# An attention kernel's norm sums, small columns and last-tile order are rearranged

## The chip, the core and the metric

The kernel runs on one core of a Trainium2 chip. The core has five engines that run side by side, each through its own list of instructions in order: TensorE (PE in the profile) multiplies matrices, VectorE (DVE) and ScalarE (ACT) work on elements, GpSimd (POOL) as well, and SyncE (SP) issues the transfers. The metric is the device time of one execution in microseconds.

## The reference

Text rows x (4 x 2048 x 512) attend to a short context (4 x 77 x 384). Cut to what matters:

```
text_p  = x @ W_text + b_text
audio_p = ctx @ W_audio + b_audio
Q = layer_norm(text_p, g1, beta1);  K = layer_norm(audio_p, g2, beta2);  V = audio_p
alpha = softmax(Q K^T / sqrt(512))
h = alpha V W_out + b_out
out = layer_norm(h + x, g_out, beta_out)
```

All is float32.

## The kernel before

Text rows are handled in 64 tiles of 128. Instead of projecting x and then multiplying with the keys, the kernel prepares one matrix for each batch entry, `mu`, which holds W_text (with its mean removed) times the scaled keys, and beside them the Gram matrix of W_text in a form that gives the square |t|^2 of the projected, centred row as a product with x itself. A tile's projection `y` (PE, L428) therefore holds the raw scores and, in further columns, the vector whose product with x is |t|^2. The Gram part of the last chunk of columns goes into a small bank of its own, `yl` (L436). The values are folded with W_out into `vw`, so that the tile's output is one product `h` (L515) of the turned weights `et` and `vw`.

The steps of a tile are named by a letter in the order lists:

- `x` turns a tile of x on DVE (L379), from a buffer `xq` that SP loads in a spread form (L178; two such buffers, each for four tiles, loaded when the tile with t == 2 begins its projection). The plain rows of x for the residual are loaded by SP too (L166, when t == 0).
- `p` and `P` are the two halves of the projection on PE. `p` does chunks 3 and 2, with `yl` after the first; `P` does 1 and 0. There are two `y` banks and two `yl` banks.
- `s` (score, DVE): adds `uws` to the scores (L463) and sums the first three chunks of |t|^2 (L452). `t` (score_rest) adds the last chunk's share from `yl` (L452), from which the final `ss` comes.
- `r` is the inverse root of |t|^2 (POOL: a maximum, L478, and a power, L209), `c` scales the scores and takes their maximum (DVE, L485 and L488), `e` the exponential (ACT, L495), `w` and `W` the transposes of the weights (PE, L507), into whichever `yl` bank the next projection will use, and their copy by ACT (L508).
- `a` is the product h (PE), `i` the reciprocal of the sum (DVE), `z` the residual sum with its row sum (DVE, L528), `q` the sum of squares (ACT, L536), `d` the inverse deviation `ro` (the scaled negative mean `nm` on ACT, L544; a multiply and add on POOL, L545; a power on POOL, L209).
- The final norm is done in one of two ways. On DVE, `v`, two operations (L559 writes an intermediate into a used `y` bank, L560 applies scale and offset and the row is stored). Or by `o` (shift `no` = nm * ro, DVE, L567), `y` (ACT, L572) and `m` (two operations of POOL, L576 and L577), after which the row is stored.

Steps r, c, e, w, i, d and o are done for a batch of tiles at once: four in most of the run, then seven batches of two and two of one. Thirteen buffers hold `z`; one comes free when its row is stored.

A front stage loads the weights, forms the keys and values in three blocks of rows (77, 128 and 103), centres W_text (`centre(k)`, k = 0 and 2 on DVE, 1 and 3 on ACT), turns it and makes the Gram matrix. `keep_warm` issues transposes of an identity matrix that have no other use. Then 40 tiles run in a regular loop, in which later steps of earlier tiles are mixed into each tile's projection (slot), and the last 24 in an order written out by hand. Every engine runs its instructions in the order in which the program emits them, SP's loads and stores included:

```
in_program_order(tc)
```

## Time and profile before

| what | value |
|---|---|
| time, median of 3 runs | 300.28 us (299.94 to 300.8) |
| the profiled execution | 301.12 us |
| its span, from first to last instruction | 299.4 us |
| mean granted TensorE clock | 0.989 |
| busy share PE / DVE / ACT / POOL | 95% / 78% / 47% / 54% |
| bytes moved | 55.58 MB, mean 186 GB/s |

The profile is of one execution. Its own time exceeds its span, as something is done around the first and last instruction. A busy share is a mean over the whole span, so stages are read by stretches. A row of the timeline has the start, the length, the engine and line, what is written and read, the shape, and in brackets how long the engine was idle before and what released it. The lines "L428" and so on are those of the kernel above; the changed kernel's lines are a few higher.

### The profile page before, as it was taken

To read this page: it belongs to the slowest core of one execution; us is meant where nothing else is said; L and a number is where in the kernel's file an instruction comes from. 1 tells how busy PE (TensorE), PEld (TensorE's weight loads), DVE (VectorE), ACT (ScalarE), POOL (GpSimd) and SP (SyncE) were. 2 spreads that over 40 slices of the span, in tenths; PEclk is the share of its full clock that TensorE was granted. 3 is DMA by queue.
4 is the path that set the end of the run, shared out by engine and by line. 5 is a ranking of instruction groups with operands and counts; after the bars stand their busy time and mean duration, and the time that the engine had idled before them with its cause. 6 is when DMAs were issued, how large, how long until landed. Compare 5 with 4: busy or idle time off the path is not lost.

```text
span 299.4 us, 3953 instructions
## 1 busy us (share of the span) xinstructions
PE 284.5 (95%) x1016; PEld 167.4 (56%) x1016; DVE 234.1 (78%) x733; ACT 139.5 (47%) x409; POOL 161.4 (54%) x188
## 2 busy tenths in 40 slices
PE   8899999999999999999999999999999999999950
PEld 6385755555555655555555555565645555556520
DVE  0593243567869798989898989889899998999985
ACT  2466210032345464636373736463656556527471
POOL 0011000010117667767585868599887887876774
PEclk9999999999999999999999999999999999999995
DMA  5999805359391878788879695969895969210315
GB/s 180 264 278 349 249 8 98 58 169 166 138 252 43 172 248 162 260 162 264 171 250 186 237 194 227 208 240 219 278 227 210 246 238 209 106 71 36 112 51 191
DMA packets 54282, 55.58 MB, mean 186 GB/s; under 512 B 2585, under 2 KB 35673, under 8 KB 54259
## 3 DMA queue, kind: packets, MB, share of 16 engines
q1 hardware_dynamic: 54259, 55.33, 68.5%
q8 instruction: 8, 0.13, 0.2%
q14 instruction: 15, 0.12, 0.1%
HBM read 38.23 MB, written 16.78 MB: 184 GB/s over the span
## 4 chain that ended last, share of the span: by engine, by line
PE 81%; DMA 6%; DVE 6%; SPq 2%; issue 1%; ACT 1%; POOL 0%; ACTq 0%; DVEq 0%
PE y L428 45%; PE h L515 17%; PE yl L436 4%; PE vw_ps L358 3%; PE m_ps L315 3%; PE et_ps L507 2%; DMA ca<-in_ctx_dram 2%; PE w_ps_yl L608 2%; DMA xq<-in_x_dram 2%; DMA out_dram<-z 2%; PE va_ps L253 2%; SPq L178 2%; DVE y L452 1%; PE w_ps_y L608 1%; DVE y L559 1%
## 5 line engine op out<-in xcount | busy, mean ns | idle before, releaser
L428 PE MATMUL y<-mu,xt 128*128 128x464 f32 (+2 forms) x512 | 178.8, 473 | 0.0
L428 PEld LDWEIGHTS y<-mu,xt 128*128 128x128 f32 x512 | 89.9, 190 | 50.0 <-issue 34.4
L515 PE MATMUL h<-vw,et 77*128 77x512 f32 x128 | 63.9, 596 | 1.3 <-ACT et L508 1.2
L536 ACT ACTIVATE sqj<-z,sz 128x512 f32<-128x512 f32 x64 | 46.1, 720 | 36.6 <-DVE z L528 33.1
L576 POOL TENSOR_TENSOR z<-z,go 128x512 f32<-128x512 f32 x44 | 55.7, 1267 | 13.8 <-ACT z L572 13.7
L577 POOL TENSOR_TENSOR z<-z,beo 128x512 f32<-128x512 f32 x44 | 55.8, 1268 | 3.4
L528 DVE SCALAR_TENSOR_TENSOR z<-h,inv,x 128x512 f32<-128x512 f32 x64 | 46.6, 733 | 2.8 <-PE h L515 1.9
L379 DVE STREAM_TRANSPOSE xt<-xq 128x512 f32<-128x512 f32 x64 | 44.6, 702 | 0.1
L452 DVE CUSTOM_DVE_ANT_1 y<-y,x,e 128x384 f32<-128x384 f32 x64 | 40.1, 626 | 2.3
L478 POOL TENSOR_SCALAR rs<-ss 128x4 f32<-128x4 f32 (+2 forms) x21 | 4.7, 223 | 68.4 <-DVE ss L452 51.3
L572 ACT ACTIVATE z<-z,no,ro 128x512 f32<-128x512 f32 x44 | 35.0, 806 | 10.4 <-DVE no L567 10.3
L436 PEld LDWEIGHTS yl<-ub,xt 128*128 128x128 f32 x128 | 23.6, 188 | 26.2 <-issue 12.6
L508 ACT COPY et<-et_ps 77x256 f32<-77x256 f32 (+1 forms) x33 | 11.9, 362 | 51.3 <-PE et_ps L507 51.3
L463 DVE TENSOR_TENSOR e<-y,uws 128x80 f32<-128x80 f32 x64 | 15.1, 235 | 18.4 <-PE y L428 18.2
L515 PEld LDWEIGHTS h<-vw,et 77*128 77x128 f32 x128 | 23.2, 190 | 10.6 <-issue 4.9
L495 ACT ACTIVATE e<-e,mx 128x77 f32<-128x77 f32 x64 | 22.2, 350 | 13.7 <-DVE mx L488 13.6
L452 DVE CUSTOM_DVE_ANT_1 yl<-yl,x,sa 128x128 f32<-128x128 f32 x64 | 22.7, 354 | 3.5
L436 PE MATMUL yl<-ub,xt 128*128 128x128 f32 x128 | 24.5, 273 | 0.0
L209 POOL TENSOR_TENSOR rs<-rs,mhalf 128x4 f32<-128x4 f32 (+2 forms) x21 | 18.6, 886 | 1.8
L209 POOL TENSOR_TENSOR ro<-ro,mhalf 128x4 f32<-128x4 f32 (+2 forms) x21 | 18.2, 867 | 1.8
L507 PEld LDWEIGHTS et_ps<-ident,e 128*77 128x77 f32 x64 | 9.1, 147 | 15.0 <-issue 9.3
L560 DVE SCALAR_TENSOR_TENSOR z<-y,ro,beo 128x512 f32<-128x512 f32 x20 | 15.0, 751 | 0.9
(102 smaller groups left out, 241.5 us busy)
## 6 DMA issues: line engine op xcount, KB each, us to landing
xq<-in_x_dram SPq DMA_DIRECT2D x64, 256.0 KB, 5.4
x<-in_x_dram SPq DMA_DIRECT2D x16, 1024.0 KB, 7.7
out_dram<-z SPq DMA_DIRECT2D x64, 256.0 KB, 2.4
wc<-in_L_xattn_W_text_dram SPq DMA_DIRECT2D x2, 512.0 KB, 8.7
wo<-in_L_xattn_W_out_dram SPq DMA_DIRECT2D x1, 1024.0 KB
wa<-in_L_xattn_W_audio_dram SPq DMA_DIRECT2D x3, 256.0 KB, 2.6
ba<-in_L_xattn_b_audio_dram SPq DMA_DIRECT2D x1, 256.0 KB, 6.7
bo<-in_L_xattn_b_out_dram SPq DMA_DIRECT2D x1, 256.0 KB
```

The costliest lines, as they stand in the source:

```text
L209: nc.gpsimd.tensor_tensor(dst, v, mhalf[: v.shape[0], : v.shape[1]], ALU.pow)
L379: nc.vector.transpose(xt.rearrange("p k (a j) -> p a k j", j=R), xq[i][:, t].rearrange("p a (k i) -> p a k i", i=R),)
L428: nc.tensor.matmul(parts(y[:, : Q * AQ])[:, :, cols], lhsT=xt[:, k, :], rhs=mub[:, k, :, cols], start=(k == LAST_K), stop=(k == 0),)
L436: nc.tensor.matmul(b, lhsT=xt[:, k, :], rhs=ub.rearrange("p q i -> p (q i)"), start=True, stop=True)
L452: nc.vector.tensor_tensor_reduce(out=y, in0=y, in1=x, scale=1.0, scalar=first, op0=ALU.mult, op1=ALU.add, accum_out=to)
L495: nc.scalar.activation(e, e, AF.Exp, bias=s.mx[:, c], accum_out=s.inv[:, c])
L515: nc.tensor.matmul(s.h[n], lhsT=s.et[:, n - s.tiles[0], :], rhs=s.vw, start=True, stop=True)
L528: nc.vector.scalar_tensor_tensor(z, s.h.pop(n), s.inv[:, c], xs[i][:, t, :], ALU.mult, ALU.add, accum_out=s.sz[:, c])
L536: nc.scalar.activation(junk, s.z[n], AF.Square, bias=s.sz[:, c], scale=-float(H), accum_out=s.sq[:, c])
L572: nc.scalar.activation(z, z, AF.Identity, bias=s.no[:, c], scale=s.ro[:, c])
L576: nc.gpsimd.tensor_tensor(z, z, go, ALU.mult)
L577: nc.gpsimd.tensor_tensor(z, z, beo, ALU.add)
```

## The change

- The first chunk of W_audio is loaded from ACT's queue. The bias `ba` is loaded after the first half of W_text, where it stood before the third key block.
- A tile of zeros, set by DVE, feeds two first matmuls; of 16 warming transposes 9 remain. The three value products, the turning of the third key block and `centre(0)` and `centre(1)` are put in another order.
- `t` becomes `score_last`: it runs during the tile's own projection, and starts its sum from `bc2` (to which H * EPS is added once), writing it into the column of `uws` that `s` then adds to the scores. `s` makes the final sum `ss`; the column `sa` goes.
- `nm` is a step `n` of its own. The multiply and add of `d` moves from POOL to ACT; the shift `no` moves from DVE to ACT, one instruction for a column.
- The norm on DVE becomes two steps, `v` and `V`, which may stand apart. If the `y` bank scored last is still in use by such a pair, the one before is used.
- The order of the last 24 tiles is rewritten. The same numbers of tiles are normed in each way (13 by DVE, 23 by ACT and POOL in that list), but partly other tiles; the loads and stores follow their steps.

```diff
@@ -129,20 +129,20 @@
     wad = w_audio.rearrange("(k p) h -> p k h", p=P)
 
     def load_audio(k):
-        nc.sync.dma_start(out=wa[:, k], in_=wad[:, k])
+        (nc.sync if k else nc.scalar).dma_start(out=wa[:, k], in_=wad[:, k])
 
     load_keys(0)
     load_audio(0)
     load_keys(1)
     for k in range(1, NA):
         load_audio(k)
-    ba = load("ba", [P, H], b_audio.partition_broadcast(P))
     for i in range(2, len(key_blocks)):
         load_keys(i)
 
     wc = xqs.tile([P, ND, T, P], F32, tag="xq", name="wc").rearrange("p k t c -> p k (t c)")
     wcd = w_text.rearrange("(k p) h -> p k h", p=P)
     nc.sync.dma_start(out=wc[:, :2], in_=wcd[:, :2])
+    ba = load("ba", [P, H], b_audio.partition_broadcast(P))
     nc.sync.dma_start(out=wc[:, 2:], in_=wcd[:, 2:])
 
     vec_rows = const.tile([3 * NH, P], F32, name="vec_rows")
@@ -190,10 +190,14 @@
     beo = load("beo", [P, H], beta_out.partition_broadcast(P))
     spread_x(1)
 
+    zeros = const.tile([P, P], F32, name="zeros")
+    nc.vector.memset(zeros, 0.0)
     ident = const.tile([P, P], F32, name="ident")
     make_identity(nc, ident)
     mhalf = const.tile([P, T], F32, name="mhalf")
     nc.gpsimd.memset(mhalf, -0.5)
+    eps = const.tile([P, 1], F32, name="eps")
+    nc.gpsimd.memset(eps, EPS)
     warm = const.tile([P, T], F32, name="warm")
     nc.scalar.activation(warm, mhalf, AF.Exp)
 
@@ -340,8 +344,7 @@
                     pu[v * HP : (v + 1) * HP].rearrange("p (b s) -> p b s", s=S),
                 )
         nc.vector.memset(uws[:, :, 0, S:], 0.0)
-        for b in range(B):
-            nc.vector.tensor_scalar_add(uws[:, b, 0, S : S + 1], bc2, H * EPS)
+        nc.vector.tensor_scalar_add(bc2, bc2, H * EPS)
 
     vw = [
         batch.tile([P if b < 2 else S, H], F32, name=f"vw_{b}") for b in range(B)
@@ -390,7 +393,7 @@
         start += size
     batch_of = {n: tiles for tiles in batches for n in tiles}
 
-    ys, state, kept, scored_y = {}, {}, [], []
+    ys, state, kept, scored_y, in_bank = {}, {}, [], [], {}
     begun = [-1]
 
     class Batch:
@@ -405,7 +408,7 @@
             def columns(name):
                 return small.tile([P, T], F32, name=f"{name}_{f}", tag=name)
 
-            self.sa, self.ss, self.rs = map(columns, ("sa", "ss", "rs"))
+            self.ss, self.rs = map(columns, ("ss", "rs"))
             self.mx, self.inv = map(columns, ("mx", "inv"))
             self.sz, self.sq, self.ro, self.nm = map(columns, ("sz", "sq", "ro", "nm"))
             self.z = {}
@@ -453,23 +456,27 @@
             out=y, in0=y, in1=x, scale=1.0, scalar=first, op0=ALU.mult, op1=ALU.add, accum_out=to
         )
 
+    def score_last(n):
+
+
+        i, t = divmod(n, T)
+        s, c = of(n)
+        yl = parts(ys[n][1])
+        sum_of_products(
+            yl, parts(xs[i][:, t, :])[:, :, LAST_K * R :], bc2, s.uw[:, 0, S : S + 1]
+        )
+
     def score(n):
 
         i, t = divmod(n, T)
-        scored_y[:] = ys[n][:1]
-        y = parts(ys[n][0][:, : Q * AQ])
+        y = ys.pop(n)[0]
+        scored_y.append(y)
+        y = parts(y[:, : Q * AQ])
         s, c = of(n)
         e = s.e[:, n - s.tiles[0], :]
         nc.vector.tensor_tensor(parts(e), y[:, :, :SQ], parts(s.uw[:, 0, :]), ALU.add)
         xp = parts(xs[i][:, t, :])[:, :, : LAST_K * R]
-        sum_of_products(y[:, :, SQ:], xp, e[:, S : S + 1], s.sa[:, c])
-
-    def score_rest(n):
-
-        i, t = divmod(n, T)
-        s, c = of(n)
-        yl = parts(ys.pop(n)[1])
-        sum_of_products(yl, parts(xs[i][:, t, :])[:, :, LAST_K * R :], s.sa[:, c], s.ss[:, c])
+        sum_of_products(y[:, :, SQ:], xp, e[:, S : S + 1], s.ss[:, c])
 
     def row_scale(f):
 
@@ -537,13 +544,16 @@
             junk, s.z[n], AF.Square, bias=s.sz[:, c], scale=-float(H), accum_out=s.sq[:, c]
         )
 
+    def minus_mean(f):
+        s = state[f]
+        nc.scalar.mul(s.nm[:, : s.m], s.sz[:, : s.m], -1.0 / H)
+
     def deviations(f):
 
         s = state[f]
         m = s.m
-        nc.scalar.mul(s.nm[:, :m], s.sz[:, :m], -1.0 / H)
-        nc.gpsimd.tensor_scalar(
-            s.ro[:, :m], s.sq[:, :m], float(H) ** -3, EPS, ALU.mult, ALU.add
+        nc.scalar.activation(
+            s.ro[:, :m], s.sq[:, :m], AF.Identity, bias=eps, scale=float(H) ** -3
         )
         rsqrt(s.ro[:, :m], s.ro[:, :m])
 
@@ -551,20 +561,26 @@
         rows = out.rearrange("b l d -> (b l) d")
         nc.sync.dma_start(out=rows[n * P : (n + 1) * P, :], in_=of(n)[0].z[n])
 
-    def norm_on_vector(n):
+    def norm_on_vector(n, step):
+
+
         s, c = of(n)
         z = s.z[n]
-
-        zc = scored_y[0]
-        nc.vector.scalar_tensor_tensor(zc, z, s.nm[:, c], kept[1] if kept else go, ALU.add, ALU.mult)
-        nc.vector.scalar_tensor_tensor(z, zc, s.ro[:, c], beo, ALU.mult, ALU.add)
-        store(n)
+        if step == 0:
+            y = scored_y[-2 if any(b is scored_y[-1] for b in in_bank.values()) else -1]
+            in_bank[n] = y
+            nc.vector.scalar_tensor_tensor(y, z, s.nm[:, c], kept[1] if kept else go, ALU.add, ALU.mult)
+        else:
+            nc.vector.scalar_tensor_tensor(z, in_bank.pop(n), s.ro[:, c], beo, ALU.mult, ALU.add)
+            store(n)
 
     def norm_shift(f):
 
         s = state[f]
         s.no = small.tile([P, T], F32, name=f"no_{f}", tag="no")
-        nc.vector.tensor_tensor(s.no[:, : s.m], s.nm[:, : s.m], s.ro[:, : s.m], ALU.mult)
+        for q in range(s.m):
+            c = slice(q, q + 1)
+            nc.scalar.mul(s.no[:, c], s.nm[:, c], s.ro[:, c])
 
     def norm_on_scalar(n):
         s, c = of(n)
@@ -622,20 +638,23 @@
         nc.vector.tensor_copy(ub if k == LAST_K else u[:, :, k * R :], p[:, :, k * R :])
         nc.gpsimd.tensor_copy(mu[1][:, k, :, SQ : SQ + m], u)
 
-    keep_warm(8)
+    for i in range(2):
+        nc.tensor.matmul(four[3][:, :P], lhsT=zeros, rhs=zeros, start=True, stop=True)
+    keep_warm(6)
     context_turned(0)
-    keep_warm(8)
+    keep_warm(3)
     pv = {0: value_product(0, [0])}
     context_turned(1)
     value_product(0, range(1, NA), pv[0])
-    context_turned(2)
+    centre(0)
+    centre(1)
     for i in range(1, NB):
-        if i > 1:
-            centre(1)
-        pv[i] = value_product(i)
+        pv[i] = value_product(i, range(2))
+        if i + 1 < NB:
+            context_turned(i + 1)
+        value_product(i, range(2, NA), pv[i])
         value(i - 1, pv[i - 1])
         if i == 1:
-            centre(0)
             statistics(0)
     centre(2)
     centre(3)
@@ -722,7 +741,7 @@
         p=begin_project,
         P=end_project,
         s=score,
-        t=score_rest,
+        t=score_last,
         r=row_scale,
         c=scale_scores,
         e=exponential,
@@ -732,11 +751,13 @@
         a=apply,
         z=residual,
         q=squares,
+        n=minus_mean,
         d=deviations,
         o=norm_shift,
         y=norm_on_scalar,
         m=norm_on_gpsimd,
-        v=norm_on_vector,
+        v=lambda n: norm_on_vector(n, 0),
+        V=lambda n: norm_on_vector(n, 1),
     )
 
     def run(steps, n):
@@ -750,13 +771,13 @@
 
     for n in range(40):
         t = n % T
-        run([("p", 0), ("s", 1), ("t", 1), ("P", 0)], n)
+        run([("p", 0), ("s", 1), ("t", 0), ("P", 0)], n)
         on_vector = t == T - 1
         if not on_vector:
             run([("o", 12)] * (t == 0) + [("y", 12)], n)
         if t == 0:
             run([("r", 4)], n)
-        run([("v" if on_vector else "m", 12)], n)
+        run([("v", 12), ("V", 12)] if on_vector else [("m", 12)], n)
         if n == KEPT:
             keep()
         else:
@@ -768,36 +789,39 @@
         run([("a", 6)], n)
         run({1: [("w", 5)], 2: [("W", 6)]}.get(t, []), n)
         run([("q", 7)], n)
-        run({0: [("e", 4)], 2: [("d", 10)]}.get(t, []), n)
+        run({0: [("e", 4)], 2: [("n", 10), ("d", 10)]}.get(t, []), n)
 
 
     for step in """
-        o28
-        p40 s39 z33 y28 y29 a34 t39 a35 r36 z34 P40 c36
-        p41 m29 s40 y31 x42 t40 P41 m31
-        p42 z35 y30 P42 q33 q34 s41 q35 e36 t41 d32 w36 m28 x43
-        p43 s42 P43 o32 t42 a36 y35 i36 v33 x44 y32 a37 s43
-        p44 x46 m30 t43 W36 P44 r40 z36 z37 a39 m32 a38 x45 c40 s44 y34 z39
-        p45 P45 t44 q37 z38 e40 x47
-        p46 q36 s45 x48 q39 P46 m35 t45 q38 s46 w40 d36 i40 o36 m34 y38
-        p47 P47 t46 W40 v36 a40 y37 s47 z40 a42 t47 a43 z42 x50 x49 a41 z41 z43 q42 q40 m38 y39
-        p48 q41 r44 P48 c44 q43 m37 s48
-        p49 d40 t48 e44 x51 w44 v43 P49 W44 a45 m39 a47 o40 s49
-        p50 y41 i44 x52 t49 m41 z45 P50 z47 a46 q45 v42 z46 a44 y40 s50 q47 z44 x53 t50 r48 q46 m40
-        p51 P51 c48 s51
-        p52 t51 q44 d44 e48 o44 y45 x54 r50 i48 m45 P52 w48
-        p53 P53 s52 a48 y46 c50 t52 e50 a49 x55 v47 m46 s53 y44 i50 z48 t53 w50
-        p54 P54 x56 q48 z49 s54 a51 a50 z51 r52
-        p55 z50 q49 m44 t54 c52 q51 x57 P55 q50 d48 d50 o48 s55 e52 i52 o50
-        p56 t55 v50 y48 w52 P56 s56 a52 m48 r54 a53 y49
-        p57 z52 m49 t56 y51 z53 c54 q52 P57 x58 q53 e54 w54
-        p58 x59 a55 d52 s57 t57 o52 P58 v52 r56 i54 c56 y53 x60
-        p59 s58 z55 t58 P59 e56 a54 w56 s59 i56 z54
-        p60 t59 m53 P60 x61 m51 a57 r58 a56 q54 q55 x62 c58 s60 d54 o54 z57 e58 y54
-        p61 z56 m54 t60 v55 q57 w58 P61 i58 q56 a59 d56 a58 s61 x63
-        p62 t61 o56 y57 P62 z58 z59 r60 m57
-        p63 q59 c60 s62 P63 e60 v56 q58 t62 s63 i60 d58 o58 w60 t63 a60 r62 c62 z60 a61 r63 y59 e62 w62 i62
-        c63 e63 a62 q60 z61 i63 w63 z62 v58 a63 q61 q62 m59 z63 d60 o60 d62 v60 v62 q63 y61 d63 m61 v63
+        s39 z33
+        p40 r36 o28 P40 x42 t40 y30 a35 z35 s40 a34 c36 y31 z34 x43
+        p41 y28 P41 m30 t41 n32 s41
+        p42 m31 P42 t42 m28 x44 q34 s42 e36 w36
+        p43 q33 x45 q35 P43 t43 a37 d32 s43
+        p44 v35 o32 r40 i36 y33 W36 V35 z37 a36 y34 y29 c40 q37 m33 P44 z36 m29 y32 a38 t44 z38 q36 x46 e40
+        p45 s44 m34 q38 a39 P45
+        p46 P46 z39 t45 n36 q39 s45 t46 d36 x47 x48 w40 i40 s46
+        p47 a41 o36 y38 v37 t47 x49 W40 z41 a40 y36 y39 V37 z40 P47 s47 a42 a43
+        p48 m32 m38 P48 q41 z42 q40
+        p49 q42 r44 x50 z43 q43 t48 n40 c44 m36 d40 s48 v41 e44 w44 P49 a45 t49 o40 x51 V41 m39 y43 a44 W44 i44
+        s49 z44 r48 z45
+        p50 t50 y42 q44 a47 x52 c48 q45 z47 P50 e48 a46 q47 m43 s50 z46 v40 m42 q46
+        p51 w48 n44 P51 t51 d44 V40
+        p52 i48 s51 v47 a49 o44 a48 x54 x53 r50 y46 P52 y45 m46 y44 V47 c50 t52 z48
+        p53 e50 z49 q48 w50 q49 P53 s52 m44 a51 t53 n48 d48 a50 s53 i50
+        p54 o48 y48 r52 x55 P54 z50 z51 m45 t54
+        p55 c52 P55 s54 n50 q51 q50 d50 m48 x57 e52 x56 w52 o50
+        p56 t55 x58 s55 P56 y51 v49 r54 i52 t56 V49 a53 x59 c54 a52
+        p57 y50 e54 z52 z53 m51 w54 P57 i54 s56 a54 a55 m50 t57
+        p58 q53 x60 s57 q52 n52 z55 d52 r56 z54 P58
+        p59 o52 t58 y52 c56 q55 s58 v53 e56 i56 q54 w56 P59 n54 a57 m52 d54 t59 o54 V53 y54 y55 s59 a56 z57 r58
+        z56 q56 q57 m54
+        p60 c58 x61 t60 P60 x62 n56 d56 e58
+        p61 s60 w58 v56 i58 t61 V56 P61 o56 a59 s61 y57 a58
+        p62 x63 P62 m55 r60 m57 z59 z58 t62 q59
+        p63 n58 c60 q58 d58 s62 v58 t63 e60 r62 w60 i60 V58 c62 o58 P63 s63 a60 e62 w62 r63 z60 i62 y59 a61 q60
+        z61 a62 n60 c63 q61 z62 e63 d60 w63 n62 a63 v60 i63 v61 V60 z63 q62 m59 V61 d62 v62 n63 v63 q63 V62 d63
+        V63
     """.split():
         do[step[0]](int(step[1:]))
 
```

## The prediction

> **What bounds the kernel now.** I read the busy shares first, then the busy time by stretch, then what PE waited for, then the chain of waits and the timeline at both ends. The page:
>
> ```profile
> PE 284.5 (95%) x1016; PEld 167.4 (56%) x1016; DVE 234.1 (78%) x733; ACT 139.5 (47%) x409; POOL 161.4 (54%) x188
> PE 81%; DMA 6%; DVE 6%; SPq 2%; issue 1%; ACT 1%; POOL 0%; ACTq 0%; DVEq 0%
> ```
>
> PE's share is an average, so the stretches decide (start:end, length, then PE, PEld, DVE, ACT, POOL busy):
>
> ```profile
> 0.00:10.00 10.00, 7.65 (x28) 4.87 (x28) 0.21 (x1) 2.32 (x4) 0.74 (x7) 1.00 0.66 225
> 150.00:180.00 30.00, 30.00 (x108) 17.82 (x107) 26.78 (x84) 15.66 (x45) 21.16 (x22) 1.00 0.82 219
> 270.00:280.00 10.00, 10.00 (x35) 5.64 (x34) 9.49 (x32) 6.02 (x18) 6.76 (x11) 1.00 0.22 82
> 290.00:299.40 9.40, 0.00 (x0) 0.00 (x0) 5.77 (x10) 2.13 (x8) 4.51 (x7) 0.66 0.45 167
> ```
>
> From about 24 us to 283 us PE has no room. Time can be won in four places only: before 24 us, in the few gaps of PE, in the last dependent steps, and behind PE's last matmul (9.4 us without PE). PE's gaps for a weight transpose are these two, at 67 and 255 us, and in front of the second stands one DVE instruction:
>
> ```profile
> 67.18 0.41 PE L507 MATMUL et_ps<-ident,e 128*77 128x128 f32 x2 [0.46 <-DVE ss L452]
> 255.81 0.41 PE L507 MATMUL et_ps<-ident,e 128*77 128x128 f32 x2 [0.72 <-DVE ss L452]
> 254.24 1.09 DVE L567 TENSOR_TENSOR no<-nm,ro 128x2 f32<-128x2 f32 x1
> 255.25 0.35 DVE L452 CUSTOM_DVE_ANT_1 yl<-yl,x,sa 128x128 f32<-128x128 f32 x1
> ```
>
> The transposes write a yl bank, which comes free only when the |t|^2 rest of the tile before has been summed; that sum stood behind a 2-column `no` of 1.09 us. The end of the chain of waits, in order of time:
>
> ```profile
> 284.79 1.99 PE h L515 x4
> 288.67 0.54 ACT sqj L536
> 290.52 0.75 DVE z L528 x2
> 292.90 0.77 DVE y L559
> 293.76 0.76 DVE z L560
> 294.62 0.77 DVE y L559
> 295.48 0.75 DVE z L560
> ```
>
> These are DVE steps of 0.75 us every 0.86 us. The last ends at 296.23, and the span 3.17 us later (store and closing).
>
> **What PE must do.** A projected tile takes 0.78 + 0.22 + 1.70 = 2.70 us (chain: "y x2", "yl x2", "y x6"), an h product 0.86, a pair of transposes 0.22. At 195.85 there are left 1.70 + 23 x 2.70 + 28 x 0.86 + 14 x 0.22 = 90.96 us, so 286.81 without a gap. Before, 4 h and 2 pairs (3.88) come after tile 63's projection, whose gapless end is 282.93; the timeline has it at 281.70 + 1.86 = 283.56. Hence 0.63 us of gaps from 195 us on. PE work is unchanged, except for five warming matmuls fewer at the start.
>
> **The change part by part.**
>
> Front. ba goes behind the third key block and wc's first half; wa's first chunk goes to ACT's queue. SP's issues ahead of those two loads fall by two and by one of 0.43 us, and ba's 256 KB no longer stand ahead of wc. At the 370 GB/s that the stretch 8 to 10 us shows, that is 0.7 us: wc's first half, first used at 11.48 now, lands about 10.8. [...] Against it: DVE's centre(0) now precedes value(0), which used to fill DVE's idle time at 9.79. From 11.48 to 22.5 DVE works almost without a break, and the key transposes of PE (22.53) wait for its last `kn`. So 0.7 us are gained and value(0)'s 0.69 are put into the row: 0. PE does two chunks of the second value product while the third key block is on its way (it idled 1.00 us at 10.33), but ACT turns that block only after centre(1) (1.75 us: 10.8 to 12.5, copied by 12.95). Its six matmuls of 0.43 end at 15.5, where PE now turns wc at 15.4 to 15.8. Front: 0, bounds -0.5 and +0.8 (wc no earlier). Fewer warming transposes: they run every 0.22 us at the start and every 0.11 at 6.56, so PE is slow until about 6 us. Were it slow until 8, six matmuls would cost 0.43 more each, in time in which PE waits for loads anyway.
>
> |t|^2 of the last chunk, summed during a tile's own projection (t beside s). Same two DVE sums per tile. The waits: t stands behind yl of its own tile, 1.2 us into the slot, while s is done after 0.9, so DVE idles up to 0.3 us, with x, z and c behind it. Per four tiles DVE's work is x 4 x 0.65, s 4 x 0.82, t 4 x 0.31, z 4 x 0.67, c 1.35, v and V 1.5: 12.7 of PE's 14.68 us, so the idle time fits. At 67 us the exponential no longer has t (0.36) in front of its norm: 0.36 of the 0.46 us gap goes. At 255 the bank is free a slot earlier and `no` is not on DVE: 0.72 shown, all within the 0.63 of gaps.
>
> Small columns by ACT. `no` leaves DVE: 19 instructions, median 159 ns, but 249 and 283 in the means (3.0 + 2.0 us) and twice 0.75 and 1.09. ACT gets 60 columns and 21 `ro`, at 0.19 alone and 0.09 in a row (two `nm`: 0.28): 8 to 15 us on 139.5 (47 to about 52%). POOL loses 21 x 0.19 = 4.0. [...] By the row of `nm` (192 ns) ACT is no dearer here than DVE's mean, and ACT is not the bound. [...] I take the row: 0 beyond the `no` counted above.
>
> Norm in two steps. Between v and V the y bank is held, so two tiles later p waits for V. Tightest: tile 40 (V40 after t51, p52 behind P51): t51 and V40 take 1.1 us from yl51, P51 leaves 1.9. Tile 47: s51, v, two x and V need 3.9 us, PE has 4.4. No stall, with 0.5 us to spare. The gain: v and V of different tiles alternate. Dependent ones stand 0.86 us apart now (292.90, 293.76, 294.62), two independent residuals 0.67 (278.25, 278.92); I take 0.70. [...]
>
> Reordered loads and stores. SP's order is that of the stores, which wait for POOL or V (13 stores waited 37.9 us for POOL's z). x47 is now turned late in slot 46, and SP, which stands at p46 with the next spread load, waits for it. Its four issues (3.4 us) and the landing (5.4 us) make 8.8 us; the first use, x52 in slot 50, is over three slots (some 12 us) later. That fits with about 3 us to spare; a store that holds SP longer than that would cost PE the excess, and is left to the range. z buffers (13) return at least five slots ahead, but for z45, which needs m32's store from slot 48.
>
> The last tiles, from the end E of tile 63's projection (its gapless end is 286.81 - 3.66 = 283.15, as transposes 60 and 61 now come before). DVE up to E has t63 done and c62 nearly (ends E + 0.25); s63 to 1.07, z60 1.74, i62 1.82, z61 2.65 (h61 at 1.95), c63 3.17, z62 3.84, v60 4.53. ACT: e62 to 0.75, its copy 1.4, y59 2.2, q60 3.0, n60 3.2, q61 4.0, and only then e63 to 4.45; so transpose 4.75, copy 5.1, h63 6.1. DVE: i63 4.65, v61 5.34, V60 6.2 (POOL's power ends 5.45), z63 6.9, V61 7.6, v62 8.3, v63 9.0, V62 9.7, V63 10.5. POOL's m59 (2.54, from 5.45 to 8.0) and both powers after it (to 9.2) precede V62 and V63. Store and closing 3.17: span = E + 13.7. Before it is 283.56 + 15.84. So the tail is 2.15 us shorter: t63, i60 and two `no` leave DVE's row (0.75), the rest is pitch and waits.
>
> Sum: E = 283.15 - 0.36 (67 us) + 0 (front) + 0.3 (gaps that I allow) = 283.1. Span 296.8 against 299.4: -2.6. The profiled execution took 301.12 (1.72 around its span), the median of three is 300.28; -2.6 on that gives 297.7.
>
> **The rivals.** First: the order of the last 24 tiles stalls PE. In slots 57 to 61 DVE has 17.1 us of work in 17.6 of PE. By my walk m52, the power for 54, r58, c58 and e58 follow each other, e58 ending at 274.25 where PE wants transpose 58 at 274.6: 0.4 us to spare. POOL's m steps are 2.54 us each; if one such step comes before the r of a batch in more places than I walked, each of nine batches can lose that. This decides from 3.5 us of added gaps (2.6 + 0.9); at 4 us the time is 301.7. For it: DVE at 9.49 of 10 and in-order queues. Against it: the old order, as tightly loaded, shows 0.63. [...] Third: everything fits, no gaps, the front gains 0.5: 296.9; or 296.3, if e63 is not held up by q61.
>
> **How the numbers follow.** About 0.3% (0.9 us) is what a measurement tells from no change: 299.4 to 301.2. The forecast with its small misses, 296.9 to 299.3: 0.62; third rival 0.12; second 0.12 (of which 0.08 lies within 0.3%, 0.04 just faster); PE stalls 0.14 (0.11 beyond 301.2, 0.03 within). So faster 0.78, same 0.11, slower 0.11. The range 296.2 to 300.8 leaves out about 0.13 above and 0.04 below.
>
> **What would show it.** Right: PE's waits at the transposes of 67 and 255 us gone, no `no` on DVE, E near 283, V63 ending near 293.5 with DVE steps 0.70 apart, span near 296.8. Wrong: wc's first use still at 11.5 and the first y later than 40.24; PE waits for y or et_ps with ACT e or DVE V as releaser between 195 and 283 us; a v to V pitch of 0.86.

## The result, and the profile after

| what | before | after |
|---|---|---|
| time, median of 4 runs each | 300.54 us (299.94 to 300.88) | 295.63 us (295.16 to 297.39) |
| ratio, 95% interval | 1 | 0.985 (0.9805 to 0.9894) |
| the profiled execution | 301.12 us | 295.41 us |
| its span | 299.4 us | 293.6 us |
| mean granted TensorE clock | 0.989 | 0.989 |

The change makes the kernel 1.5% faster, 4.9 us where 2.6 were forecast. The predicted 297.7 us is 2.1 us too long, and the measured time lies 0.6 us below the range. The direction was right, the size was not. The profiled pair differs by 5.7 us; what it has above the 4.9 is no more than the first stage varies by from one execution to the next (below).

The first part of the page of after, and its fourth, the shares of the chain that ended last:

```profile
PE 283.5 (97%) x1013; PEld 167.5 (57%) x1013; DVE 226.9 (77%) x712; ACT 154.6 (53%) x490; POOL 157.3 (54%) x168
PE 94%; DVE 3%; DMA 1%; issue 1%; DVEq 0%; ACT 0%
```

PE's busy time has hardly changed (283.5 against 284.5); its share of the chain has gone from 81 to 94%, while DMA fell from 6 to 1% and DVE from 6 to 3%: what went is waiting. (The shares say where the chain runs. 13% of the span is far more than was gained.) ACT is 15 us busier. The busy time by stretch in after (start:end, length, then PE, PEld, DVE, ACT, POOL, granted clock, DMA share, GB/s):

```profile
0.00:10.00 10.00, 8.59 (x28) 5.20 (x29) 0.85 (x2) 3.03 (x6) 0.77 (x8) 1.00 0.81 259
150.00:180.00 30.00, 30.00 (x107) 17.60 (x107) 25.83 (x84) 17.31 (x56) 20.76 (x20) 1.00 0.79 223
270.00:280.00 10.00, 10.00 (x38) 6.01 (x38) 9.18 (x30) 5.64 (x23) 8.53 (x11) 1.00 0.29 107
290.00:293.60 3.60, 0.00 (x0) 0.00 (x0) 0.58 (x1) 0.00 (x0) 0.00 (x0) 0.50 0.51 189
```

The first 10 us move 259 GB/s in place of 225. The middle is as full of PE as before. After 290 us only 3.6 us are left, of which 0.58 are DVE's, where before had 9.4 us. The transpose of the first weights, in the timeline of after, has lost its bracket, so PE did not wait there:

```profile
65.31 0.38 PE L514 MATMUL et_ps<-ident,e 128*77 128x128 f32 x2
```

and from 24 us to the end the waits of PE by releaser (total us, times, longest) are two, both for ACT and both behind tile 63's projection:

```profile
PE et_ps L514 <- ACT e L502: 1.1, 1, 1.1
PE h L522 <- ACT et L515: 0.4, 1, 0.4
```

To find where the 5.8 us of span came from, I cut the span at PE's `yl` products, one at the start of each tile's projection: they stand in every kernel here, and the work of PE between the same two of them is the same in all. Five stages result. Each row is one profiled execution, in us:

| kernel | first yl | to yl of tile 6 | 6 to 40 | 40 to 63 | 63 to end | span |
|---|---|---|---|---|---|---|
| before | 40.86 | 27.35 | 124.75 | 88.52 | 17.9 | 299.4 |
| after | 39.61 | 26.70 | 124.75 | 87.05 | 15.5 | 293.6 |
| b0_before_again | 39.90 | 27.35 | 124.76 | 88.52 | 17.9 | 298.4 |
| b1_bias_late | 40.46 | 27.35 | 124.75 | 88.55 | 17.9 | 299.0 |
| b2_first_weights_by_act | 41.32 | 27.35 | 124.76 | 88.56 | 17.9 | 299.9 |
| b3_both_loads | 39.32 | 27.36 | 124.75 | 88.52 | 17.9 | 297.8 |
| b4_front_order | 40.95 | 27.36 | 124.75 | 88.52 | 17.8 | 299.4 |
| b5_plain_load_in_place | 40.41 | 27.35 | 124.75 | 88.52 | 17.8 | 298.8 |
| b6_rest_in_own_projection_only | 40.44 | 26.70 | 124.76 | 90.78 | 17.9 | 300.6 |
| b7_rest_later_in_slot_57 | 40.85 | 26.71 | 124.75 | 88.96 | 17.9 | 299.2 |
| a1_rest_after_score | 39.18 | 27.34 | 124.75 | 90.90 | 15.8 | 298.0 |
| a2_shift_on_dve | 39.71 | 26.71 | 124.74 | 88.78 | 16.7 | 296.6 |
| a3_norm_steps_together | 39.44 | 26.70 | 124.75 | 87.81 | 17.2 | 295.9 |
| a4_old_list | 38.70 | 26.70 | 124.75 | 91.98 | 20.7 | 302.8 |
| a8_old_list_shift_on_dve | 39.70 | 26.70 | 124.75 | 95.71 | 18.5 | 305.4 |
| a5_last_exponential_first | 39.32 | 26.70 | 124.75 | 87.05 | 16.2 | 294.0 |
| a6_old_front_order_too | 40.38 | 26.70 | 124.75 | 87.05 | 16.1 | 295.0 |

From before to after the front gains 1.25, the first weights 0.65, the last 24 tiles 1.47 and the end 2.4. The middle stage repeats to 0.02 us over all 17 rows, and the stages of before repeat as well, but for the first: it varies by about 0.5 us either way from one execution to the next. Three kernels have time in their rows in which PE still had work and ran at a granted clock of 0.50: a8 in the last 24 tiles, a2 and a4 at the end (told there; in a5 it is 0.1 us).

### The profile page after: what moved, and what is told of

Read it like the earlier page. It is cut to its first block, busy times and chain, and to the rows that moved or that the text cites. A ratio compares the mean times of both kernels' runs of the same rounds, so it can differ in the third digit from the quotient of the medians.

```text
span 293.6 us, 3970 instructions
## 1 busy us (share of the span) xinstructions
PE 283.5 (97%) x1013; PEld 167.5 (57%) x1013; DVE 226.9 (77%) x712; ACT 154.6 (53%) x490; POOL 157.3 (54%) x168
## 4 chain that ended last, share of the span: by engine, by line
PE 94%; DVE 3%; DMA 1%; issue 1%; DVEq 0%; ACT 0%
PE y L431 53%; PE h L522 18%; PE yl L439 5%; PE vw_ps L361 4%; PE va_ps L257 3%; PE m_ps L319 3%; PE et_ps L514 2%; PE w_ps_yl L624 2%; DMA ca<-in_ctx_dram 1%; PE w_ps_y L624 1%; DVE z L574 1%; PE uw_ps L337 1%; DVE z L535 1%; DVE y L572 1%; PE cat_ps L246 1%
## 5 line engine op out<-in xcount | busy, mean ns | idle before, releaser
L455 DVE CUSTOM_DVE_ANT_1 yl<-yl,x,bc 128x128 f32<-128x128 f32 x64 | 22.6, 353 | 28.2 <-PE yl L439 28.0
L572 DVE SCALAR_TENSOR_TENSOR y<-z,nm,gain_ps 128x512 f32<-128x512 f32 x20 | 14.9, 751 | 0.8
```

Source lines behind the costliest of these rows:

```text
L455: nc.vector.tensor_tensor_reduce(out=y, in0=y, in1=x, scale=1.0, scalar=first, op0=ALU.mult, op1=ALU.add, accum_out=to)
```

## The experiments

Kernels named b are before with one piece of the change; those named a are after with one piece taken back.

### The front: b1, b2, b3, b4, b5 and b0

In after, `wc` is first used at 9.29 us; the forecast had 10.8. b1 moves the bias alone:

```diff
-    ba = load("ba", [P, H], b_audio.partition_broadcast(P))
     for i in range(2, len(key_blocks)):
         load_keys(i)
     ...
     nc.sync.dma_start(out=wc[:, :2], in_=wcd[:, :2])
+    ba = load("ba", [P, H], b_audio.partition_broadcast(P))
```

> The kernel before, with one edit: the load of ba moved behind the first half of wc. Theory A (ba's transfer holds up what stands behind it): wc's first use by ACT falls from 11.48 us to below 10, the rate between 5 and 8 us rises from about 210 to over 300 GB/s; but value(0) stands ahead of centre(0) on DVE and waits for ba (about 10.6), so the first yl product moves only to 40.6 to 41.0 (now 40.86). Theory B (only the number of issues on SP counts): wc's first use at 11.0 or later. Theory C (the earlier wc alone carries the front's gain): first yl at 39.6 to 39.9.

b2 moves only W_audio's first chunk to ACT's queue, `(nc.sync if k else nc.scalar)` in `load_audio`, and b3 does both:

> The kernel before, with one edit: the first chunk of wa is loaded from ACT's queue. Theory A: the queue saves one issue (0.4 us) and little else; wc's first use at 11.0 to 11.5, first yl at 40.4 to 40.9. Theory B (a second queue lets the transfers run beside each other and is what won the front): wc's first use at 9.3 to 10, first yl at 39.6 to 40.1.

> The kernel before with both load edits and the old order of the front's operations. Theory A: wc's first use at 9.3 to 9.8 as in the changed kernel (9.29), but DVE waits for ba ahead of centre(0), so that the first yl is at 40.2 to 40.9: the order is needed to cash in the earlier load. Theory C: the loads alone give 39.6 to 39.9.

b4 has before's loads and the new order of the front's work (zeros, fewer warming transposes, the third key block turned inside the second value product, `centre(0)` and `centre(1)` ahead of it):

> The kernel before with the new order of the front's operations (zeros, fewer warming transposes, value products split, both centrings first) and the old loads. Theory A: wc still comes at about 11.4, value(0) is now behind centre(0), and the third block's copy behind centre(1), so that the first yl moves back to 41.4 to 41.7. Theory D (the order itself won the front): first yl at 39.6 to 40.3.

Two rows show what the bias does. The stretch of 5 to 8 us, before first, then b1:

```profile
5.00:8.00 3.00, 2.91 (x9) 1.14 (x8) 0.00 (x0) 0.48 (x1) 0.00 (x0) 1.00 0.66 213
```

```profile
5.00:8.00 3.00, 3.00 (x11) 1.36 (x11) 0.00 (x0) 0.48 (x1) 0.00 (x0) 1.00 0.97 324
```

The last column is GB/s: with the bias among the early loads the queues move 213, without it 324, and the DMA engines' busy share goes from 0.66 to 0.97. ACT's first use of `wc`, in the timelines of before and then of b1, moves by 1.6 us:

```profile
11.48 0.63 ACT L587 ACTIVATE wc<-wc 128x512 f32<-128x512 f32 x1 [0.24 <-DMA wc<-in_L_xattn_W_text_dram]
```

```profile
9.89 0.63 ACT L587 ACTIVATE wc<-wc 128x512 f32<-128x512 f32 x1 [0.83 <-DMA wc<-in_L_xattn_W_text_dram]
...
10.66 0.69 DVE L262 TENSOR_TENSOR va<-va_ps,ba 77x512 f32<-77x512 f32 x1 [10.66 <-DMA ba<-in_L_xattn_b_audio_dram]
```

In the six executions with the bias early and `wc` behind it (before, b0, b2, b4, b6, b7) that use lies between 10.55 and 11.60, 11.16 on the mean, so the move is 1.3 us on the mean, where 256 KB take 0.7 us at the 375 GB/s of before's stretch from 8 to 10 us. The other row of b1 is the price: `value(0)` now waits for the bias, until 10.66, and b1's first yl, 40.46, is no earlier than before's. b2 alone leaves the rate at 228 GB/s and the use of `wc` at 11.60; b3 has 330 and 9.14; b4 229 and 11.03, and PE waits 1.32 us at 13.10 for ACT's copy of the third key block, the wait that the prediction had foreseen for the new order.

Is it the bytes of the bias, or the way in which it is loaded? It is one row of 2 KB read 128 times, once for each partition. b5 puts a plain load of the same 256 KB (the last quarter of `wc`) in its place, and the bias where b1 has it:

```diff
-    ba = load("ba", [P, H], b_audio.partition_broadcast(P))
+    nc.sync.dma_start(out=wc[:, 3:], in_=wcd[:, 3:])
     ...
     nc.sync.dma_start(out=wc[:, :2], in_=wcd[:, :2])
-    nc.sync.dma_start(out=wc[:, 2:], in_=wcd[:, 2:])
+    ba = load("ba", [P, H], b_audio.partition_broadcast(P))
+    nc.sync.dma_start(out=wc[:, 2:3], in_=wcd[:, 2:3])
```

> The kernel before with a plain load of 256 KB (the last quarter of wc) in the place of ba, and ba behind the first half of wc; the rest of wc after it. Theory A1 (ba's repeated reading of one row is what slows the transfers): rate between 5 and 8 us over 290 GB/s, wc's first half used by ACT at 10.0 to 10.7. Theory A2 (any 256 KB there do it, by their bytes alone): rate as before (about 210), first use at 11.2 to 11.6.

Measured: 284 GB/s from 5 to 8 us, just under what was expected, and `wc` used by ACT at 9.82 although as many bytes stand ahead of it as in before. So most of the delay is the kind of load: as 128 reads of one row it holds up what is queued with it (213 GB/s in before, 284 here). Why, the runs don't show. b0 is before once more, with nothing changed:

> The kernel before, unchanged, profiled once more: how far does a stage's time vary from one execution to the next? The front of the changed kernel put the first yl product at 39.61, 39.18, 39.71, 39.44 and 38.70 us in five profiles. Expected: 40.4 to 41.3 for the first yl (now 40.86), and from there to tile 63's yl the same 240.6 us within 0.1.

It measures the stage's own spread, which is wider than expected: first yl 39.90 against 40.86, `wc` at 10.55 against 11.48, 239 GB/s. By groups, the first yl is at 40.86, 39.90, 40.44 and 40.85 with the old loads and the old order (mean 40.51, with b6 and b7), and at 39.61, 39.18, 39.71, 39.44, 38.70, 39.70 and 39.32 with both new (mean 39.38): 1.1 us. The new order on the old loads gives 40.95, no gain; the new loads on the old order 39.32 and 40.38. So both loads together are needed, either alone showed no gain in its one execution (b1, b2), and what the order adds to them can't be told from the spread. The expectation of b3 that the order is needed to cash in the earlier load is not borne out.

### The |t|^2 sum: a1, b6 and b7

a1 is after with the sum behind the score of the same tile again, in the hand-written list too (`s41 t41`), and the column `sa` back:

```diff
-        run([("p", 0), ("s", 1), ("t", 0), ("P", 0)], n)
+        run([("p", 0), ("s", 1), ("t", 1), ("P", 0)], n)
```

> The changed kernel with the last chunk's sum back behind each tile's score (t after s of the same tile, as before). Theory A (the exponential's chain and the yl bank were what the first gap and part of the later ones waited for): the 0.65 us at the first weight transposes comes back (yl of tile 6 stands 0.65 later against yl of tile 5), and 0.4 to 1.5 us of gaps appear from tile 41 on, as transposes wait for DVE sums; span 294.7 to 296. Theory B (the order of the last tiles did it all): only the 0.65 comes back, span 294.2 to 294.5.

The stage to tile 6 is back at 27.34, all of the 0.65, and the last 24 tiles lose 3.85, more than either theory had. The waits of PE in a1 from 195 to 290 us name the bank again:

```profile
PE et_ps L512 <- DVE ss L456: 2.3, 2, 1.2
PE et_ps L512 <- DVE z L533: 0.8, 1, 0.8
```

Is the moved sum then worth 4.5 us by itself? b6 is before with only this moved, in the old order of the last 24, each `t` at the earliest place that is free, behind its own `p` and the `s` before it:

> The kernel before, with one thing changed: the last chunk's share of |t|^2 is summed during its own tile's projection, all 64 tiles, in the old order of the last 24. Theory A: that alone brings the 0.65 us at the first weight transpose (the first yl to tile 6's, against before) and takes away the gap at 255 us; yl40 to yl63 then takes 87.8 to 88.5 us against 88.52, and with a front of before's the span is 297.9 to 299.1. Theory B: DVE, standing at t until yl has been written, hands its x, z and c on late, and the old list has no room for it; then yl40 to yl63 is 89 us or more and the span 299.4 or more.

The 0.65 at tile 6 is there (26.70), but the last 24 tiles are 2.3 us longer than before's. The timelines of DVE and of PE in b6 show where:

```profile
259.11 0.36 DVE L451 CUSTOM_DVE_ANT_1 yl<-yl,x,bc 128x128 f32<-128x128 f32 x1 [1.45 <-PE yl L435]
```

```profile
262.29 0.68 PE L510 MATMUL et_ps<-ident,e 128*77 128x128 f32 x2 [1.63 <-ACT e L498]
```

DVE reaches `t57` before PE has written the bank and stands for 1.45 us; two residuals and the scaled scores are queued behind it, so the exponential is late and PE waits 1.63. This is the wait that the prediction had taken for "up to 0.3 us" and fitting. b7 moves one step of b6:

```diff
-        p57 t57 z52 m49 y51 z53 c54 q52 P57 ...
+        p57 z52 m49 y51 z53 c54 t57 q52 P57 ...
```

> The kernel of b6 (before, with the last chunk's |t|^2 summed in its own projection) with one step moved: in the slot of tile 57, t57 goes from straight behind p57 to behind c54, so that two residuals and the scaled scores no longer stand behind its wait for PE. Theory A: that wait is what made b6's list stall; the gap of 1.63 us before the transpose at 262 us goes, b6's loss between the yl of tiles 56 and 58 (9.64 us against 8.47 in before) is not there, the yl of tiles 40 to 63 are 87.8 to 88.6 us apart, and with the tail of before the span is 299.0 to 299.8 less what the front gains or loses against b6's. Theory B: t57 late pushes s57 or z back and the gap only moves: yl40 to yl63 stays above 90 us.

The gap is gone: from the yl of tile 56 to that of tile 58 PE takes 7.81 us, against 9.64 in b6 and 8.47 in before. The 88.96 of the whole stage is a little above what was expected, since 0.27 in slot 40 and 0.86 in slot 50 are still lost. So the moved sum alone is worth the 0.65 at tile 6; in the last 24 tiles it takes away before's gap at 255 us (0.91 us less from the yl of tile 56 to that of tile 57), but in the old order it costs 0.44 more than that elsewhere. After's list has its `t57` behind `z52` and `z53` as well.

### The small columns: a2

```diff
-        for q in range(s.m):
-            c = slice(q, q + 1)
-            nc.scalar.mul(s.no[:, c], s.nm[:, c], s.ro[:, c])
+        nc.vector.tensor_tensor(s.no[:, : s.m], s.nm[:, : s.m], s.ro[:, : s.m], ALU.mult)
```

> The changed kernel with the shift no on DVE again, one instruction for a batch. Theory A (long no instructions stall the queue that PE waits for): 18 or 19 no at a median of 0.16 us, with one to three of 0.5 to 1.1 us; DVE has 3 to 5 us more, the regular loop does not move, and 0.2 to 1.0 us are lost in the last 24 tiles or the tail; span 293.8 to 294.8. [...]

With `no` on DVE the last 24 tiles take 1.73 us longer and the end 1.2, together more than was expected. Most of the end's 1.2 is not a wait: PE's last two products, in the timelines of a2 and then of after, run at half clock in a2 (granted clock 0.52 on the mean from 287.4 to 289.5 us) and take 0.93 us longer.

```profile
287.44 2.06 PE L522 MATMUL h<-vw,et 77*128 77x512 f32 x2 [0.35 <-ACT et L515]
```

```profile
285.36 1.13 PE L522 MATMUL h<-vw,et 77*128 77x512 f32 x2 [0.35 <-ACT et L515]
```

In after the clock falls too, but 0.8 us behind PE's last product. So some 1.9 of the 2.9 us are what `no` itself costs. The largest piece of them, 0.84 in slot 60, is behind a `no` of normal length, in a2's timelines of DVE and PE: DVE stands 1.34 us ahead of it for POOL's power, and PE then waits for a tile of x that DVE turns late.

```profile
267.25 0.16 DVE L581 TENSOR_TENSOR no<-nm,ro 128x2 f32<-128x2 f32 x1 [1.34 <-POOL ro L213]
```

```profile
271.75 1.02 PE L431 MATMUL y<-mu,xt 128*128 128x464 f32 x2 [0.60 <-DVE xt L382]
```

Other pieces, as the 0.52 in slot 47, are behind a `no` that is itself long. The group of `no` has a median of 160 ns and a longest of 1257. Some of the long ones begin while a wide operation of POOL runs and end within 0.02 us of it, at 217.4 and at 252.2 us (timelines of a2, DVE, then POOL):

```profile
216.17 1.26 DVE L581 TENSOR_TENSOR no<-nm,ro 128x4 f32<-128x4 f32 x1
...
251.15 1.11 DVE L581 TENSOR_TENSOR no<-nm,ro 128x2 f32<-128x2 f32 x1
```

```profile
216.15 1.26 POOL L591 TENSOR_TENSOR z<-z,beo 128x512 f32<-128x512 f32 x1
...
250.97 1.27 POOL L590 TENSOR_TENSOR z<-z,go 128x512 f32<-128x512 f32 x1
```

### The norm in two steps: a3

Each `v` is put straight in front of its `V`, and no other step moves:

```diff
-        z61 a62 n60 c63 q61 z62 e63 d60 w63 n62 a63 v60 i63 v61 V60 z63 q62 m59 V61 d62 v62 n63 v63 q63 V62 d63
-        V63
+        z61 a62 n60 c63 q61 z62 e63 d60 w63 n62 a63 i63 v60 V60 z63 q62 m59 v61 V61 d62 n63 q63 v62 V62 d63
+        v63 V63
```

> The changed kernel with v moved to stand directly ahead of its V everywhere. Theory A (dependent DVE steps stand 0.86 us apart, alternating ones 0.70): the end of tile 63's projection does not move (280.4) and the tail behind it is 0.5 to 1.1 us longer; span 294.1 to 294.7. [...] Theory C: holding v back to V's place makes DVE wait and PE stall in the last 24 tiles, span over 295.

The end is 1.7 us longer, the last 24 tiles 0.76. The last DVE steps in a3's timeline, then in after's:

```profile
289.58 0.76 DVE L572 SCALAR_TENSOR_TENSOR y<-z,nm,gain_ps 128x512 f32<-128x512 f32 x1
290.44 0.75 DVE L574 SCALAR_TENSOR_TENSOR z<-y,ro,beo 128x512 f32<-128x512 f32 x1
291.30 0.76 DVE L572 SCALAR_TENSOR_TENSOR y<-z,nm,gain_ps 128x512 f32<-128x512 f32 x1
292.16 0.75 DVE L574 SCALAR_TENSOR_TENSOR z<-y,ro,beo 128x512 f32<-128x512 f32 x1
```

```profile
287.87 1.41 DVE L572 SCALAR_TENSOR_TENSOR y<-z,nm,gain_ps 128x512 f32<-128x512 f32 x2
289.18 1.40 DVE L574 SCALAR_TENSOR_TENSOR z<-y,ro,beo 128x512 f32<-128x512 f32 x2
```

In a3 each of these steps depends on the one before: `V` reads what `v` wrote, and the next `v` writes the bank that this `V` reads. Such steps start 0.86 us apart. In after two `v` and then two `V` stand in a row: 289.18 - 287.87 = 1.31 for two, 0.66 each. This pitch makes up 0.9 of the end's 1.7 us. Another 0.7 is one step more behind `z63`: `v61`, which in after fills time ahead of it, now stands behind it, so that six steps follow and not five.

### The old order of the last 24 tiles: a4 and a8

a4 is after with before's list, `t` at the earliest free place, `n` in front of `d` and each `V` behind its `v`:

> The changed kernel with the old order of the last 24 tiles (t of each tile put into its own projection, each v followed by its V, each d preceded by n). Theory A (the order of the last tiles has most of the 1.47 us between tile 40 and tile 63 and of the tail): yl of tile 63 against yl of tile 40 at 88.0 to 88.5 (before 88.52, changed 87.05), tail behind tile 63's projection 14.8 to 15.6 (before 15.84, changed 13.2), span 296 to 297.5. Theory B (the moved operations did it, whatever the order): 87.0 to 87.4 and a tail of 13.2 to 14, span 293.6 to 294.8.

At 302.8 us it is 9.2 longer than after, and longer than before, which neither theory had. Near the end the chain's steps, in a4's timeline, are

```profile
284.36 0.71 POOL L213 TENSOR_TENSOR ro<-ro,mhalf 128x2 f32<-128x2 f32 x1 [1.88 <-ACT ro L555]
...
285.10 0.48 ACT L583 ACTIVATE no<-nm,ro 128x1 f32<-128x1 f32 x2 [0.82 <-POOL ro L213]
...
285.89 1.12 PE L522 MATMUL h<-vw,et 77*128 77x512 f32 x2 [1.46 <-ACT et L515]
```

ACT waits for POOL's power with `no` at the head of its queue, and the copy of the weights, which PE needs, stands behind it. Behind this wait, from about 288.5 us, PE has a granted clock of 0.50 while it works, and its last two pairs of products take 1.94 and 2.08 us, where a8's take 1.13 and 1.12: 1.8 us of a4's end. The stretch of a4 (third column from the right):

```profile
288.50:293.00 4.50, 4.07 (x5) 0.96 (x5) 2.81 (x8) 3.11 (x11) 1.18 (x2) 0.50 0.00 0
```

To see whether `no` on ACT makes the old order lose, a8 puts `no` back on DVE in a4, as a2 does in after:

> The changed kernel with the old order of its last 24 tiles, and with the shift no on DVE in one instruction, as before; t still in its tile's own projection and the norm in two steps, the second straight behind the first. Theory A: in the old list ACT's queue stands at the shift, which waits for POOL's power, and the weights' copies and exponentials stand behind it; with the shift on DVE that goes. PE from yl40 to yl63 then takes 87.8 to 89.0 us (against 91.98 with the shift on ACT), the tail behind tile 63's projection 15 to 16 us, the span 297 to 299.5. Theory B: it is t, standing in its own projection and so waiting for yl, or the norm, that makes the old list stall; then yl40 to yl63 stays above 91 and the span above 301.5.

The wait of 1.46 is down to 0.46, as theory A has it, and in slot 56 a8 is 1.2 us faster than a4; but the span is 305.4. (The end is 2.2 us shorter than in a4, 18.5 against 20.7, and most of that is a4's clock.) The stall for `t57` is in a8 as in b6 (9.63 us from yl 56 to yl 58), and there is a new one at 219 us. The four columns of `no` wait 1.02 us for POOL's power there and then take 1.23 us, PE waits 0.43 and then 0.97 for what follows on ACT and DVE, and then runs at half its clock (stretches of a8; the third column from the right is the granted clock):

```profile
219.00:223.00 4.00, 2.59 (x5) 0.91 (x5) 3.93 (x11) 1.91 (x4) 3.84 (x5) 0.91 0.86 235
223.00:229.00 6.00, 6.00 (x10) 2.71 (x10) 3.65 (x13) 3.91 (x11) 4.01 (x4) 0.50 0.78 262
229.00:233.00 4.00, 4.00 (x18) 2.73 (x18) 2.99 (x9) 1.85 (x9) 2.93 (x3) 0.98 0.00 0
```

From the yl of tile 47 to that of tile 49 a8 takes 14.37 us against 9.49 in a4. Of these 4.9 us, 1.4 are the two waits; the other 3.5 agree with half of the roughly 7 us at half clock. Without the drops a8 would be at about 302 and a4 at about 301, by this estimate. So the old order, with the changed steps put in where they are here, loses at `t57` whichever engine does `no`; with `no` on ACT it loses 1.2 more just before (10.86 us from yl 56 to yl 58 in a4) and 1.0 in the wait at the end, with `no` on DVE the 1.4 at 219 us and what the clock then took. The old order with `t57` where b7 has it and the other changed steps was not run.

### A better end: a5 and a6

In after the last exponential, `e63`, stands behind `q61` on ACT. a5 puts it ahead of `q61` and `d60`, and `z63` ahead of `V60`:

```diff
-        z61 a62 n60 c63 q61 z62 e63 d60 w63 n62 a63 v60 i63 v61 V60 z63 q62 ...
+        z61 a62 c63 e63 n60 z62 q61 w63 d60 n62 a63 v60 i63 v61 z63 V60 q62 ...
```

> The changed kernel with e63 moved ahead of q61 and d60, and z63 ahead of V60. Theory A (PE waits 1.15 us for this exponential, behind q61, and z63 and the last norm hang on it): transposes of 63 about 0.3 us earlier, tail behind tile 63's projection 12.8 to 13.0 in place of 13.2; ratio to before 0.984. Theory B (DVE's row of steps is the bound of the tail anyway, or the later ro60 takes it back): tail 13.1 to 13.4.

295.97 us (ratio to before 0.9844, 0.9815 to 0.9873): no different from after. PE waits 0.8 in place of 1.1 us for that exponential, but then 0.6 in place of 0.35 for the copy of its weights, which now stands behind `q61`, so the last product ends no earlier: 6.12 us behind tile 63's projection, against 6.08. The end is 16.2 against 15.5, and DVE's row shows why:

```profile
286.27 0.75 DVE L535 SCALAR_TENSOR_TENSOR z<-h,inv,x 128x512 f32<-128x512 f32 x1 [0.66 <-PE h L522]
...
286.95 1.41 DVE L574 SCALAR_TENSOR_TENSOR z<-y,ro,beo 128x512 f32<-128x512 f32 x2
288.27 1.41 DVE L572 SCALAR_TENSOR_TENSOR y<-z,nm,gain_ps 128x512 f32<-128x512 f32 x2
289.58 1.41 DVE L574 SCALAR_TENSOR_TENSOR z<-y,ro,beo 128x512 f32<-128x512 f32 x2
```

`z63` waits 0.66 us for that product with nothing to do, and `V60`, which fills this time in after, comes behind it. From there six norm steps follow without a gap, one more than in after, at 0.66 us each. The later power for tile 60 (it begins 5.11 us behind the projection, against 4.48) may have cost something had `V60` kept its place; in this row it holds nothing up.

a6 adds the old order of the front (with the new loads) to a5:

> As the run before it, and the front's operations in the old order (16 warming transposes, third block turned ahead, value(0) ahead of centre(0)) with the new loads. Theory A (the loads won the front, the order is worth nothing): first yl at 38.7 to 39.7 as with the new order; span within 0.4 us of the run before. Theory D (the order gave a part): first yl at 40 or later.

296.98 us (0.9888, 0.9849 to 0.9927), the intervals of both overlapping; the first yl is 1.06 later than in a5, about the spread of that stage. No version here beats after.

## Why the prediction was wrong, step by step

The predicted span was 296.8, the measured one 293.6: 3.2 us. Five terms make it up, all in one direction. The first two, the load of `ba` and the sum of PE's work, are the steps that failed.

- **"Front: 0."** It gained 1.25 in the profiled pair, and 1.1 on means. The mis-sized term is the load of `ba`: I charged 256 KB at 370 GB/s (the trace has 375), 0.7 us, and this load takes more than its bytes from what is queued with it (213 against 324 GB/s in b1). With `wc` 2.2 us earlier in the profiled pair and not 0.7, the 0.69 of `value(0)` that I put into DVE's row no longer uses up the gain. For the load moved to ACT's queue I counted no more than one issue of 0.43 us on SP, and that stands: b2 by itself shows no gain (first yl 41.32, against 40.86). The wait for the third key block came as described, in b4, which lacks the new loads; in after that copy stands at 11.30.
- **"Hence 0.63 us of gaps from 195 us on."** The step that failed is the sum of PE's work, 90.96. It begins with the row "195.85 1.70 PE y x6", taken for the rest of one projection. It is not: a tile has eight such matmuls, two ahead of `yl`. The chain of before:

```profile
193.35 0.78 PE y L428 x2
194.13 1.72 PE h L515 x4
195.85 1.70 PE y L428 x6
197.54 0.22 PE yl L436 x2
```

The two at 193.35 belong to tile 40, as do four of the six at 195.85 (0.92); the other two there are the next tile's first (0.78), which the 23 x 2.70 hold already. The sum is 0.78 too long, and so before had 1.41 us of gaps there, not 0.63. In its stage from yl 40 to yl 63, 88.52, the work by the same rows is 87.10; after takes 87.05, so all gaps went. An added 0.78 to "what PE must do" hid more than half of what there was to win.
- **"0.36 of the 0.46 us gap goes"** at 67 us. 0.65 went, in after, in b6 and in b7: all of the wait and not a part. The bracket of 0.46 also counts from the end shown for the matmul before, and the next one otherwise begins about 0.17 us ahead of that end (a row of after starts at 64.68, lasts 0.80, and the transposes start at 65.31). 0.46 + 0.17 is 0.63.
- **"0.3 (gaps that I allow)"**: none came, except behind the last projection.
- **"Span = E + 13.7."** E is the end of tile 63's projection, 279.33 + 1.08 = 280.41 in after, so the end took 13.2; before 15.84. Right to 0.5 us, and by the steps named: `e63` did come behind `q61` (PE's one wait of 1.1 us), the pitch was 0.66 for 0.70, `V63` ended 10.17 behind E for 10.5.

1.25 + 0.29 + 0.78 + 0.36 (the gaps allowed, and rounding) + 0.5 is the 3.2.

Two values were taken from rows of before. The first is the pitch, 0.70. Dependent steps stand at 0.86 us (before, a3), independent ones at 0.66 (after, a5), and a3 shows what having all at 0.86 costs at the end, 0.9 us. The row of before, 0.67 for two independent residuals, was the good guide. The second is the time of `no` on ACT, for which I took the row of `nm`, and I put the move at "0 beyond the `no` counted above". By the time of one instruction DVE is the cheaper place: a `no` takes 0.16 us there at the median, for up to four columns, and on ACT, in after, 0.28 for one column and 0.20 more for each that follows at once (I had 0.19 and 0.09). What pays is to have its waits off DVE: a2 shows some 1.9 us in this list, and the row does not show the reason. The wait for yl, which the prediction had as harmless, is so in the new list; a4, a8 and b6 show that it isn't in the old one.

That the parts hang together is what the sum could not show. Taken out of after one at a time they cost 4.8 us (a1, of its 4.4 us in the span and an earlier front of 0.43), 2.9 (a2, of which about 1.0 is the clock) and 2.5 (a3, with its own front taken off in the same way), the list 10.1 (a4, 1.8 of it the clock); the first alone, put into before, gives 0.65 and takes 2.3 (b6), or 0.44 with one step moved (b7). The first rival, that the order of the last 24 stalls PE, was the right worry about the wrong order: the changed steps stall in the old one, as it was filled in for a4.

## What to carry to other kernels

Before forecasting what filling gaps is worth, count the bound engine's instructions between two marks in the trace and not from a row of the chain, since a row may join two steps; hold the sum against a stage with no gaps (here 2.70 a tile). In a hand-written order price an operation together with its place: a step that waits for PE is free only if nothing urgent is queued behind it (`t57` in two places: from the yl of tile 56 to that of tile 58 9.64 us in b6, 7.81 in b7). Look at what kind of load stands ahead of a first use, not only at its bytes (256 KB both times: 213 GB/s beside the bias in before, 284 beside b5's plain load). And before a longer stage is put down to a wait, read the granted clock of that stretch (0.50 from 223 to 229 us in a8).

## What was not expected of the hardware

- A load that reads one 2 KB row 128 times slowed its neighbours: 207 to 239 GB/s from 5 to 8 us in the six executions with it early, 297 to 330 in the ten with it late, and 284 with a plain load of the same size in its place (b5, one execution).
- A `no` on DVE that began beside a wide operation of POOL (L576 or L577 in before) ended with that operation. In the profiles of before, a2 and a8, ten `no` began while such an operation of 1.27 us ran, and all ten ended within 0.02 us after its end (in a2 217.43 against 217.41, 252.26 against 252.24), whether 2 or 4 columns wide; all the others took 0.12 to 0.16. DVE's residuals were not held: 0.74 us at the median in before, both for the 25 that began in such an operation and for the other 39. What sets `no` apart from them the runs don't show. This is one reason why a step of 0.16 us at the median took up to 1.26 on DVE, and it is absent on ACT, where the 60 `no` of after take 0.28 to 0.30 each; the other cost of `no` on DVE is that it waits for POOL's power at the head of DVE's queue, 1.34 us in a2's slot 60.
- In a8 two waits of PE of 0.43 and 0.97 us, 1 us of work apart, were followed by about 7 us at a granted clock of 0.50; in a4 waits of 1.46 and 0.35 us by half clock from 288.5 us on, in a2 waits of 1.07 and 0.35 from 287.5 on. After has waits of 1.15 and 0.35 at the same place, and its clock held until PE was done; single waits of 1.63 (b6) and 1.57 us (a4, a8) cost no clock either. Even with one kernel the moment differs: behind tile 63's projection the clock fell after 9.4 us in before and after 7.2 in b0. What decides it the runs don't show.
- The front of one and the same kernel moves by about half a microsecond either way from one execution to another, everything after it by 0.1 at most in the executions of before and of the kernels that differ from it in the front alone.
